# Attention, then a mixture of experts: the experts' rows in turns of 768 and 256 instead of 512 and 512

## The chip, the core and the metric

The kernel runs on one core of a Trainium2 chip. The core has five engines with an instruction queue each: PE (matrix multiplications), DVE (vector work), ACT (activation functions and copies), POOL (here above all the issuer of gathers and scatters by row number) and SP (issuer of plain transfers). Each queue is worked off in order; an instruction that has to wait holds all that stands behind it in its queue. Sixteen DMA engines move data between the large memory (HBM) and the core's own memory. [...]

The metric is the device time of one execution in microseconds (us). Twelve runs of the kernel before took 1091.36 to 1098.12 us, 1096.07 us in the median.

## What is computed

The input is x, 4 batches of 1024 rows of 256 numbers. The layer is causal attention with 16 heads, a layer norm, a mixture of experts, and another layer norm. The attention takes the first two thirds of the time and is not touched by the change. The part that matters, from the reference:

```python
scores = (jnp.einsum('btd,ed->bte', x, router_w) + router_b) / temp
gates = _sinkhorn(scores)                  # three rounds over experts and over rows of a batch
topk_vals, topk_idx = jax.lax.top_k(gates, K)          # K = 2 of E = 8 experts
topk_gates = topk_vals / (jnp.sum(topk_vals, axis=-1, keepdims=True) + 1e-08)
g = jax.nn.relu(jnp.einsum('btd,edf->btef', x, wg))    # 256 -> 512
p = jnp.einsum('btd,edf->btef', x, wp)                 # 256 -> 512
all_out = jnp.einsum('btef,efd->bted', g * p, wo)      # 512 -> 256
...
x = _layernorm(x + expert_out)
```

Each row goes to two experts, so there are 8192 pairs of a row and an expert, 1024 for each expert on average. The normalisation of the gates runs over all rows of a batch: who goes where in a batch is known only when the attention of the whole batch is done.

## The kernel before, in words

**Lists of pairs.** The kernel computes each pair only for the expert that wants it. After the attention of a batch, `finish` writes its normed rows to `x1_rows` in HBM (and, as the start of the sum, to `results`), and `route` works out gates and experts: many small steps on DVE, ACT and PE, one after the other. Then `route` scatters the pairs into a list in HBM, `pairs`, with 16 indirect transfers of 128 pairs on POOL (L842). The list has a region of `REGION` entries for each expert; an entry holds the row number, the row to add to, and the gate. `base` holds for each expert where its next pair goes. After the third batch of four, `base` is raised to `floor` where it is below it (L826), the end of the expert's first slot: what comes after it in the region is from then on pairs of the last batch, or pairs beyond the first slot.

**Slots.** A slot is a number of list entries of one expert that are worked on together. There are 8 first slots of ER = 512 entries (`Slot(0, e)`), 8 second slots of 512 (`Slot(1, e)`, in reverse order), and further slots of SR = 256 entries for what an expert has beyond 1024. How many further slots are needed, and where they lie, is worked out on the chip (`lay_out`); `SURE` = 3 of them are always run, and a branch runs all others when more than 3 are needed. Empty entries point to spare rows. The first slots need only pairs and rows of three batches (`x1_rows[: BT - T]`), so they can start, and be worked on, while the last batch is still being routed.

**One slot.** `gather` fetches the rows of a slot with one indirect transfer for 128 rows on POOL (L950), into one of two `xg` buffers. [...] `weights` loads three matrices of 512 KB from SP (L970) into one buffer each, and `halves` splits them with six copies on ACT (L190) and six subtractions on DVE (L191), into one of two buffers. `slot` then makes four blocks of gate and lin (`gp`, `lp`), each of 128 hidden columns, applies relu and product (L1006, L1007), splits the hidden block (`hh`, `hl`) and multiplies it with the third matrix into `eo`, 128 rows at a time. ACT copies `eo` out with the gate as scale (L1023) into one of six buffers, and POOL adds it to `results` with an indirect transfer (L1024). Two slots may hold the same row, so every add of a slot waits until all adds of the slot before it have landed (`after`, `added`). The second turn begins with the expert that the first turn ended with, and takes its split weights (`like`).

**The order.** `begin(keys, n, ...)` is a generator with the preparation of slot n: gathers for slot n + 1, `rows` for slot n, and three steps of `halves` and the next slot's `weights`; `slot` advances it between its blocks, so that slot n is prepared while slot n - 1 is computed. These instructions, and the small steps of the last batch's `route`, are then ordered within each engine's queue by a planner that the framework runs at build time. `begin_early` puts the first slot's loads ahead of the end of the attention.

**After the experts.** `results` is loaded again in 8 pieces (L1229), normed by DVE, POOL and ACT, and stored (L1232).

Of the kernel before, what the change touches and what calls it, by code (L numbers as in the profile page):

```python
# [14 lines left out]
ALU = mybir.AluOpType  # L15
# [11 lines left out]
SURE = 3  # L27
# [8 lines left out]
P = 128  # L36
# [7 lines left out]
def kernel(  # L44
# [38 lines left out]
    ER = 512  # L83
    SR = 256
    REGION = BT + SR
    NOVER = (2 * BT - 4 * ER + 2 * (SR - 1)) // SR
    NLIST = (E - 1) * REGION + 2 * ER + NOVER * SR
    NLIST += -NLIST % P

# [407 lines left out]
    for e in range(E):  # L497
        nc.gpsimd.memset(rank[:, e : e + 1], float(E - e))
        nc.gpsimd.memset(base[:, e : e + 1], float(e * REGION))
        nc.gpsimd.memset(floor[:, e : e + 1], float(e * REGION + ER))  # L500
    ones = const.tile([P, P], F32, name="ones")
# [354 lines left out]
    for e in range(E):  # L856
        nc.gpsimd.memset(shift[:, e : e + 1], float(e * REGION + 2 * ER - SR + 1))
    tables = {}

    def lay_out():  # L860
# [31 lines left out]
        nc.vector.scalar_tensor_tensor(table[:, 1], slot_no, float(SR), table[:, 1], ALU.mult, ALU.add)  # L892
        nc.vector.tensor_scalar(table[:, 1], table[:, 1], float(2 * ER), None, ALU.add)
        tables["slots"] = small.tile([1, 2, NOVER], I32, tag="ti", name="ti", bufs=1)
# [21 lines left out]
    class Slot:  # L916


        def __init__(self, which, s):
            self.which, self.s, self.name = which, s, f"{which}_{s}"  # L920
            self.rows = SR if which == 2 else ER
            self.blocks = self.rows // P
            self.raw, self.hl = [None] * 3, [None] * 3
            self.like = None

    lists = {}

    def pairs_of(k):
        if k.which == 2:
            row = value(1, k.s, NLIST - SR)  # L930
            k.ent = const.tile([P, k.blocks, 4], I32, name=f"ent_{k.name}")
            nc.sync.dma_start(
                out=k.ent, in_=pairs[bass.ds(row, SR)].rearrange("(p j) w -> p j w", j=k.blocks)
            )
            return
        if k.which not in lists:
# [3 lines left out]
                out=ent.rearrange("p e j w -> p e (j w)"),  # L940
                in_=regions[:, k.which * ER : (k.which + 1) * ER].rearrange("e (p j) w -> p e (j w)", p=P),
            )
            if not k.which:
                apart("pairs", "early", ins, ("last",))
        k.ent = lists[k.which][:, k.s]

    def gather(k):
        k.xg = early.tile([P, ER // P, C], F32, tag="xg", name=f"xg{k.name}", bufs=XG)
        for j in range(k.blocks):
            ins = nc.gpsimd.indirect_dma_start(  # L950
                out=k.xg[:, j], out_offset=None, in_=x1_rows[: BT if k.which else BT - T],
                in_offset=bass.IndirectOffsetOnAxis(ap=k.ent[:, j, 0:1], axis=0),
            )
            if not k.which:
                in_turn(ins)
                apart("x1", "early", ins, ("last",))

    def weights(k, i):

        if k.like is not None:  # L960
            return
        if k.which == 2:
            if i == 0:
# [8 lines left out]
    def halves(k, i):  # L972
        if k.like is not None:
            k.hl[i] = k.like.hl[i]
            return
        w = k.raw[i]
# [15 lines left out]
    def slot(k, between):  # L992

        R = k.rows
        hs = []
        for f in range(NFC):
            cut = slice(f * P, (f + 1) * P)
            if 2 * R > QC:
                gate, lin = (mx_tile(f"{i}p{k.name}_{f}") for i in "gl")
            else:  # L1000
                both = mx_tile(f"gp{k.name}_{f}")
                gate, lin = both[:, :R], both[:, R:]
            for (h_, l_), ps in zip(k.hl, (gate, lin)):
                mm3(ps, [(h_[:, c, cut], l_[:, c, cut], k.xh[:, c, :R], k.xl[:, c, :R]) for c in range(CC)])
# [9 lines left out]
        mine = []  # L1014
        h_, l_ = k.hl[2]
        for j in range(k.blocks):
# [11 lines left out]
            apart(f"results{k.name}", "add", ins, ("add",))  # L1028
            if not k.which:
                apart("results", "early", ins, ("last",))  # L1030
# [64 lines left out]
    budget = {0: (8.0, 8.0, 8.0, 11.3), 1: (9.5, 9.5, 6.0, 11.3), 2: (9.5, 9.5, 6.0, 0.0)}  # L1095
    first = [Slot(0, e) for e in range(E)]
    second = [Slot(1, e) for e in reversed(range(E))]
    second[0].like = first[-1]
    further = [Slot(2, n) for n in range(NOVER)]
    early = None  # L1100

    def begin_early():
        pairs_of(first[0])
        for i in range(3):
# [98 lines left out]
    def run(keys, given=()):  # L1203
# [4 lines left out]
    run(first + second + further[:SURE], (0,))  # L1208

# [133 lines left out]
```

## Time and profile before

| what | value |
|---|---|
| median of 12 runs | 1096.07 us (1091.36 to 1098.12) |
| the profiled execution | 1102.4 us, of which its span is 1100.7 us |
| PE busy | 985.3 us, 90% of the span, 6392 matmuls |
| DVE busy | 736.7 us, 67% |
| ACT busy | 626.2 us, 57% |
| POOL busy | 481.5 us, 44% |
| moved by DMA | 119.66 MB, 109 GB/s on average |
| first slot's rows transposed | from 721 us |
| last matmul of the experts | 1065 us |
| reload of `results` begins | 1075 us |

The profile is one execution. A line of a window gives start and end, its length, and then for PE, PEld (the loading of weights into PE), DVE, ACT and POOL the busy us with the number of instructions, the clock that PE was granted (1.00 is full speed), the share of time in which the DMA engines were busy, and GB/s. A line of the timeline gives start, duration, engine, line of the code, operation, tile written <- tiles read, size and count, and in brackets how long the engine had been idle and what ended that. Matmuls overlap, so the distance from one start to the next is what a matmul costs, not its duration. "remote" in such a bracket is a wait whose end the profile gives to no instruction of this core, as with transfers by POOL. The chain of waits gives start, length and what it was, followed back from the last instruction.

### The profile page before, as it was taken

To read this page: it belongs to the slowest core of one execution; us is meant where nothing else is said; L and a number is where in the kernel's file an instruction comes from. 1 tells how busy PE (TensorE), PEld (TensorE's weight loads), DVE (VectorE), ACT (ScalarE), POOL (GpSimd) and SP (SyncE) were. 2 spreads that over 40 slices of the span, in tenths; PEclk is the share of its full clock that TensorE was granted. 3 is DMA by queue.
4 is the path that set the end of the run, shared out by engine and by line. 5 is a ranking of instruction groups with operands and counts; after the bars stand their busy time and mean duration, and the time that the engine had idled before them with its cause. 6 is when DMAs were issued, how large, how long until landed. Compare 5 with 4: busy or idle time off the path is not lost.

```text
span 1100.7 us, 18000 instructions
## 1 busy us (share of the span) xinstructions
PE 985.3 (90%) x6392; PEld 606.9 (55%) x6392; DVE 736.7 (67%) x1630; ACT 626.2 (57%) x1314; POOL 481.5 (44%) x551
## 2 busy tenths in 40 slices
PE   6689999999999898999899799899999699999960
PEld 4455433455535244544345333278888488888860
DVE  3777787888888586788438688275676355646636
ACT  3455766765665564676566467665654354656633
POOL 6176511122443623351423301754566865653544
PEclk9899999999999898999999899999999699999985
DMA  6573420231230321323133220166573545665647
GB/s 237 167 221 116 116 98 19 63 116 57 75 115 31 93 69 49 125 66 109 50 97 105 45 63 2 21 214 167 111 177 74 122 89 151 137 152 108 155 61 305
DMA packets 71362, 119.66 MB, mean 109 GB/s; under 512 B 16416, under 2 KB 43040, under 8 KB 70880
## 3 DMA queue, kind: packets, MB, share of 16 engines
q1 hardware_dynamic: 48544, 81.76, 23.4%
q0 software_dynamic: 20672, 36.41, 15.3%
q8 instruction: 52, 0.85, 0.3%
q10 hardware_dynamic: 2048, 0.27, 0.2%
q14 instruction: 46, 0.38, 0.1%
HBM read 82.52 MB, written 35.60 MB: 107 GB/s over the span
## 4 chain that ended last, share of the span: by engine, by line
PE 74%; DVE 6%; ACT 6%; DMA 5%; issue 3%; SPq 2%; another core or an unknown queue 2%; POOL 1%; ACTq 0%; DVEq 0%; POOLq 0%
PE y L437 13%; PE s L353 11%; PE sT L456 10%; PE gp L198 3%; PE gp L199 3%; PE gp L197 3%; PE eo L197 3%; PE eo L198 3%; ACT pT L462 3%; PE eo L199 3%; PE lp L199 2%; PE lp L198 2%; PE lp L197 2%; PE po L623 2%; PE s L370 2%
## 5 line engine op out<-in xcount | busy, mean ns | idle before, releaser
L462 ACT ACTIVATE pT<-sT 128x512 f32<-128x512 f32 (+1 forms) x608 | 326.7, 576 | 184.2 <-PE sT L456 135.8
L374 DVE TENSOR_REDUCE mx<-s 128x1 f32<-128x384 f32 (+3 forms) x352 | 216.4, 632 | 63.3 <-PE s L370 45.4
L456 PE MATMUL sT<-qs,ks 98*128 98x512 bf16 (+3 forms) x768 | 216.1, 333 | 26.8 <-ACT pT L462 17.4
L353 PE MATMUL s<-ks,qs 96*128 96x512 bf16 (+3 forms) x768 | 213.0, 333 | 14.2 <-DMA ks<-parts 7.7
L474 POOL TENSOR_SCALAR_AFFINE_SELECT pT<-pT 128x512 f32<-128x512 f32 x120 | 75.8, 637 | 289.8 <-ACT pT L462 267.0
L383 DVE TENSOR_REDUCE mx<-s 128x1 f32<-128x512 f32 x256 | 171.0, 679 | 36.8 <-PE s L353 34.7
L437 PE MATMUL y<-pT,va 128*32 128x512 f32 (+3 forms) x1536 | 177.5, 510 | 3.0 <-issue 2.2
L1024 POOL DMA_INDIRECT results<-eo,ents x64 | 104.4, 1632 | 91.8 <-ACT eo L1023 68.9
L353 PEld LDWEIGHTS <-qs 96*128 96x128 bf16 x768 | 71.4, 100 | 123.3 <-issue 96.1
L456 PEld LDWEIGHTS <-ks 98*128 98x128 bf16 x768 | 69.5, 99 | 98.5 <-issue 65.4
L197 PE MATMUL eo<-wh,hh 128*128 128x256 f32 x280 | 81.9, 294 | 6.5 <-ACT eo L1023 6.5
L370 PE MATMUL s<-mask,ident_b 128*128 128x128 bf16 (+2 forms) x352 | 87.5, 249 | 0.0
L191 DVE TENSOR_TENSOR wl<-w,wh 128x512 fp32r<-128x512 f32 x108 | 69.6, 683 | 26.5 <-ACT wh L190 18.6
L1007 DVE TENSOR_TENSOR relu<-relu,lp 128x512 f32<-128x512 f32 x64 | 43.7, 683 | 64.7 <-PE lp L199 24.6
L842 POOL DMA_INDIRECT pairs<-ent,so_i x64 | 66.8, 1043 | 33.1 <-issue 18.1
L198 PE MATMUL eo<-wl,hh 128*128 128x256 f32 x280 | 80.2, 288 | 0.0
L1006 ACT ACTIVATE relu<-gp 128x512 f32<-128x512 f32 (+1 forms) x76 | 42.8, 563 | 65.7 <-PE gp L199 39.9
L950 POOL DMA_INDIRECT xg<-x_rows,ents x64 | 65.4, 1021 | 31.7 <-issue 17.4
L199 PE MATMUL eo<-wh,hl 128*128 128x256 f32 x280 | 78.0, 285 | 0.0
L437 PEld LDWEIGHTS y<-pT,va 128*32 128x32 f32 x1536 | 32.5, 109 | 68.4 <-issue 54.0
L191 DVE TENSOR_TENSOR hl<-relu,hh 128x512 fp32r<-128x512 f32 (+1 forms) x76 | 48.5, 645 | 29.1 <-ACT hh L190 19.9
L197 PE MATMUL gp<-xh,wh 128*128 128x512 f32 (+1 forms) x176 | 64.2, 371 | 3.3 <-DVE relu L1007 1.8
(212 smaller groups left out, 1852.0 us busy)
## 6 DMA issues: line engine op xcount, KB each, us to landing
ks<-parts SPq DMA_DIRECT2D x90, 128.0 KB
w<-in_wg_dram SPq DMA_DIRECT2D x18, 512.0 KB
w<-in_wp_dram SPq DMA_DIRECT2D x18, 512.0 KB
w<-in_wo_dram SPq DMA_DIRECT2D x18, 512.0 KB
qs<-parts SPq DMA_DIRECT2D x66, 128.0 KB
parts<-lv POOLq DMA_DIRECT2D x12, 384.0 KB
parts<-lv POOLq DMA_DIRECT2D x24, 192.0 KB
xh<-in_x_t_dram SPq DMA_DIRECT2D x8, 512.0 KB
```

Source lines behind the costliest of these rows:

```text
L191: (sub or nc.vector).tensor_tensor(lo, src, hi.bitcast(F32), ALU.subtract)
L197: nc.tensor.matmul(ps, lhsT=sh, rhs=mh, start=(i == 0), stop=False)
L198: nc.tensor.matmul(ps, lhsT=sh, rhs=ml, start=False, stop=False)
L199: nc.tensor.matmul(ps, lhsT=sl, rhs=mh, start=False, stop=(i == n - 1))
L353: nc.tensor.matmul(ps, lhsT=q(h, half)[:NROW, t * P : (t + 1) * P], rhs=k(h, kc)[:NROW, :w], start=first, stop=last,)
L370: nc.tensor.matmul(each[:, :, w - P :], lhsT=ident_b, rhs=mask.unsqueeze(1).to_broadcast([P, m, P]), start=False, stop=True,)
L374: nc.vector.tensor_reduce(mx_of[:, half, h0 : h0 + m, t], each, AX.X, ALU.max)
L383: nc.vector.tensor_reduce(mx_of[:, kc, h, t : t + 1], ps, AX.X, ALU.max)
L437: nc.tensor.matmul(acc[g, qc][SLOT * h : SLOT * (h + 1), lo:], lhsT=va[b % 2][:, kb, at : at + SLOT], rhs=pT[:, h, lo:], start=(kb == 0), ...
L456: nc.tensor.matmul(st[:, h % m * w : (h % m + 1) * w], lhsT=k(h, kb // BPQ)[: NROW + 2, kb % BPQ * P : (kb % BPQ + 1) * P], rhs=q(h, qc)[: ...
L462: nc.scalar.activation(pT[:, h + 1 - m : h + 1, lo:], st[:, : m * w].rearrange("p (h t) -> p h t", t=w), AF.Exp, scale=scale,)
L1024: ins = nc.gpsimd.indirect_dma_start(out=results[:, :], out_offset=bass.IndirectOffsetOnAxis(ap=k.ent[:, j, 1:2], axis=0), in_=eo, in_offs ...
```

## The change

The regions of the list, the slots and their order change; the mathematics and the number of pairs don't.

- The first turn takes 768 entries of each expert, as two slots: `Slot(0, e)` with entries 0 to 511 and `Slot(1, e)` with entries 512 to 767. The second of them has `like` set to the first and uses its split weights. Both draw on the rows of three batches only.
- The second turn takes 256 entries, 768 to 1023, as `Slot(2, e)`, in reverse order of the experts. The first of these uses the weights of the last expert of the first turn, as before.
- The further slots are `Slot(3, n)`, 256 entries as before, beyond 1024.
- `floor` is raised from entry 512 to entry 768 of each region. `FIXED`, the number of entries in the fixed slots, is 1024 as `2 * ER` was.
- `pairs_of` loads a list for each of the three kinds of fixed slots. Two of them are loaded early, `begin_early` does so for the first two slots.
- `begin` gathers for the next slot in all cases, and looks for the next slot with weights of its own: its `halves` are made in the slot before it, unless they are there already, and the weights after that are loaded.

In all there are 8 slots of 512 and 16 of 256 entries, and 3 further ones, where there were 16 of 512 and 3 further ones. [...]

```diff
+    FIXED = ER + 2 * SR
     REGION = BT + SR
-    NOVER = (2 * BT - 4 * ER + 2 * (SR - 1)) // SR
-    NLIST = (E - 1) * REGION + 2 * ER + NOVER * SR
+    NOVER = (2 * BT - 2 * FIXED + 2 * (SR - 1)) // SR
+    NLIST = (E - 1) * REGION + FIXED + NOVER * SR
...
-        nc.gpsimd.memset(floor[:, e : e + 1], float(e * REGION + ER))
+        nc.gpsimd.memset(floor[:, e : e + 1], float(e * REGION + ER + SR))
...
-            self.rows = SR if which == 2 else ER
+            self.at, self.rows = ((0, ER), (ER, SR), (ER + SR, SR), (None, SR))[which]
...
-                in_=regions[:, k.which * ER : (k.which + 1) * ER].rearrange("e (p j) w -> p e (j w)", p=P),
-            )
-            if not k.which:
+                in_=regions[:, k.at : k.at + k.rows].rearrange("e (p j) w -> p e (j w)", p=P),
+            )
+            if k.which < 2:
                 apart("pairs", "early", ins, ("last",))
...
     def weights(k, i):
-        if k.like is not None:
-            return
...
     def halves(k, i):
-        if k.like is not None:
-            k.hl[i] = k.like.hl[i]
-            return
...
+        hl = (k.like or k).hl
...
-    first = [Slot(0, e) for e in range(E)]
-    second = [Slot(1, e) for e in reversed(range(E))]
-    second[0].like = first[-1]
-    further = [Slot(2, n) for n in range(NOVER)]
+    first = [Slot(which, e) for e in range(E) for which in range(2)]
+    for a, b in zip(first[::2], first[1::2]):
+        b.like = a
+    second = [Slot(2, e) for e in reversed(range(E))]
+    second[0].like = first[-2]
+    further = [Slot(3, n) for n in range(NOVER)]
...
     def begin_early():
-        pairs_of(first[0])
+        for k in first[:2]:
+            pairs_of(k)
...
         k, nxt = keys[n], keys[n + 1] if n + 1 < len(keys) else None
-        early_next = nxt is not None and (nxt.which == 0 or k.which > 0)
-        if n not in given and (k.which and (n == 0 or not keys[n - 1].which)):
+        if n == 0 and not given:
             pairs_of(k)
             gather(k)
-        if early_next:
-            pairs_of(nxt)
+            for i in range(3):
+                weights(k, i)
+        if nxt is not None:
+            if nxt.ent is None:
+                pairs_of(nxt)
             gather(nxt)
-        if n not in given:
-            if n == 0:
-                for i in range(3):
-                    weights(k, i)
+        if n or not given:
             rows(k, st_tile)
+        own = [m for m in keys[n:] if m.like is None][:2]
         for i in range(3):
-            halves(k, i)
-            if nxt is not None:
-                weights(nxt, i)
+            if own and own[0].hl[i] is None:
+                halves(own[0], i)
+                if len(own) > 1:
+                    weights(own[1], i)
             yield
```

More of the change, by code (lines that the diff above doesn't have):

```diff
@@ L856 @@
     for e in range(E):
-        nc.gpsimd.memset(shift[:, e : e + 1], float(e * REGION + 2 * ER - SR + 1))
+        nc.gpsimd.memset(shift[:, e : e + 1], float(e * REGION + FIXED - SR + 1))
     tables = {}
@@ L892, in lay_out @@
         nc.vector.scalar_tensor_tensor(table[:, 1], slot_no, float(SR), table[:, 1], ALU.mult, ALU.add)
-        nc.vector.tensor_scalar(table[:, 1], table[:, 1], float(2 * ER), None, ALU.add)
+        nc.vector.tensor_scalar(table[:, 1], table[:, 1], float(FIXED), None, ALU.add)
         tables["slots"] = small.tile([1, 2, NOVER], I32, tag="ti", name="ti", bufs=1)
@@ L920, in __init__ @@
             self.which, self.s, self.name = which, s, f"{which}_{s}"
-            self.rows = SR if which == 2 else ER
+            self.at, self.rows = ((0, ER), (ER, SR), (ER + SR, SR), (None, SR))[which]
             self.blocks = self.rows // P
             self.raw, self.hl = [None] * 3, [None] * 3
+            self.ent = None
             self.like = None
@@ L928, in pairs_of @@
     def pairs_of(k):
-        if k.which == 2:
+        if k.which == 3:
             row = value(1, k.s, NLIST - SR)
@@ L950, in gather @@
             ins = nc.gpsimd.indirect_dma_start(
-                out=k.xg[:, j], out_offset=None, in_=x1_rows[: BT if k.which else BT - T],
+                out=k.xg[:, j], out_offset=None, in_=x1_rows[: BT - T if k.which < 2 else BT],
                 in_offset=bass.IndirectOffsetOnAxis(ap=k.ent[:, j, 0:1], axis=0),
             )
-            if not k.which:
+            if k.which < 2:
                 in_turn(ins)
@@ L958, in weights @@
     def weights(k, i):
-        if k.like is not None:
-            return
-        if k.which == 2:
+        if k.which == 3:
             if i == 0:
@@ L1002, in slot @@
                 gate, lin = both[:, :R], both[:, R:]
-            for (h_, l_), ps in zip(k.hl, (gate, lin)):
+            for (h_, l_), ps in zip(hl, (gate, lin)):
                 mm3(ps, [(h_[:, c, cut], l_[:, c, cut], k.xh[:, c, :R], k.xl[:, c, :R]) for c in range(CC)])
@@ L1014, in slot @@
         mine = []
-        h_, l_ = k.hl[2]
+        h_, l_ = hl[2]
         for j in range(k.blocks):
@@ L1028, in slot @@
             apart(f"results{k.name}", "add", ins, ("add",))
-            if not k.which:
+            if k.which < 2:
                 apart("results", "early", ins, ("last",))
@@ L1184, in begin, with run @@
         k, nxt = keys[n], keys[n + 1] if n + 1 < len(keys) else None
-        early_next = nxt is not None and (nxt.which == 0 or k.which > 0)
-        if n not in given and (k.which and (n == 0 or not keys[n - 1].which)):
+        if n == 0 and not given:
             pairs_of(k)
             gather(k)
-        if early_next:
-            pairs_of(nxt)
+            for i in range(3):
[3 more added lines that the diff above has]
+                pairs_of(nxt)
             gather(nxt)
-        if n not in given:
-            if n == 0:
-                for i in range(3):
-                    weights(k, i)
+        if n or not given:
             rows(k, st_tile)
+        own = [m for m in keys[n:] if m.like is None][:2]
         for i in range(3):
-            halves(k, i)
-            if nxt is not None:
-                weights(nxt, i)
+            if own and own[0].hl[i] is None:
+                halves(own[0], i)
+                if len(own) > 1:
+                    weights(own[1], i)
             yield
-    def run(keys, given=()):
+    def run(keys, given=False):
         drain(begin(keys, 0, given))
@@ L1206, in run @@
             slot(key, begin(keys, n + 1, given))
-    run(first + second + further[:SURE], (0,))
+    run(first + second + further[:SURE], True)
     experts.close()
```

## The prediction

> **What bounds the kernel now.** I read the page's busy shares first (PE 90% of 1100.7 us), then, since the change touches only the experts, windows over the expert stage, the timeline across its one hole, and POOL's and SP's queues. As built, the two programs agree on every engine up to the first transposes of gathered rows at 721 us, so only what follows can move. The windows (PE, PEld, DVE, ACT, POOL busy; then granted clock, DMA share, GB/s):
>
> ```profile
> 835.00:857.00 22.00, 20.26 (x119) 16.89 (x117) 10.54 (x21) 8.51 (x18) 17.43 (x16) 1.00 0.28 75
> 857.00:866.00 9.00, 2.47 (x10) 2.00 (x9) 1.98 (x3) 2.55 (x6) 7.17 (x7) 0.63 0.43 67
> 866.00:876.00 10.00, 7.17 (x23) 5.62 (x24) 4.47 (x7) 3.27 (x7) 8.47 (x6) 0.50 0.90 226
> ...
> 900.00:937.00 37.00, 37.00 (x217) 32.50 (x217) 20.33 (x32) 19.63 (x39) 19.18 (x16) 1.00 0.56 128
> ...
> 1030.00:1040.00 10.00, 9.98 (x83) 9.73 (x81) 6.46 (x14) 5.81 (x15) 3.47 (x3) 1.00 0.68 199
> ```
>
> PE is full in both turns and in the further slots (1030 on). The hole is 835 to 876: 1.74 + 6.53 + 2.83 = 11.1 us of idle PE, and about 9.6 busy us at half clock, worth 4.8 us more: **15.9 us** in all. The timeline says whose hole it is:
>
> ```profile
> 856.47 0.96 POOL L842 DMA_INDIRECT pairs<-ent,so_i  x1 [0.30 <-issue]
> 857.73 1.93 POOL L1024 DMA_INDIRECT results<-eo,ents  x1 [0.30 <-issue]
> 858.82 0.37 SPq L939 DMA_DIRECT2D ents<-pairs  x1
> ...
> 862.55 0.47 ACT L1023 ACTIVATE eo<-eo,ents 128x256 f32<-128x256 f32 x1 [5.11 <-remote]
> ...
> 863.08 0.58 PE L197 MATMUL eo<-wh,hh 128*128 128x256 f32 x1 [5.90 <-ACT eo L1023]
> ...
> 864.89 0.37 SPq L970 DMA_DIRECT2D w<-in_wo_dram  x1
> ```
>
> From 833.89 to 857.43 POOL issues the last batch's sixteen scatters of pairs (23.5 us), with the adds of results queued behind them. All six `eo` buffers fill, ACT's copy waits until the first delayed add has landed (857.73 to 862.55, 4.8 us), and PE waits for ACT. SP stands at the load of `ents` from 840 to 858.8, so no weights arrive either.
>
> **The change, part by part.** *The sizes.* I counted the pairs of each expert with the reference on its inputs: 719, 701, 714, 777, 783, 739, 912, 799 from three batches, and 233, 236, 231, 243, 268, 256, 307, 274 from the last. With a floor of 512 or of 768, three experts pass 1024 and need one further slot each, so three further slots run in both kernels. Rows (8960) and weight loads (18 of each matrix) stay. Eight 512-row slots become sixteen of 256.
>
> *Narrower matmuls, on the path.* PE's timeline, start to start:
>
> ```profile
> 1023.03 0.39 PE L197 MATMUL gp<-xh,wh 128*128 128x512 f32 x1
> 1023.25 0.39 PE L198 MATMUL gp<-xl,wh 128*128 128x512 f32 x1
> ...
> 1031.93 0.28 PE L198 MATMUL gp<-xl,wh 128*128 128x256 f32 x1
> 1032.05 0.28 PE L199 MATMUL gp<-xh,wl 128*128 128x256 f32 x1
> ```
>
> A 512-wide matmul takes 0.228 us, a 256-wide one 0.120. A 512-row slot has 48 of them for gate and lin; two slots of 256 have 96: 48 x (0.240 - 0.228) = 0.56 us, times 8 = **+4.5 us**. The output matmuls (256 wide before, too) and the transposes keep their number. ACT and DVE get some 80 instructions more each and run beside PE.
>
> *The hole, smaller but not gone.* In POOL's built queue the sixteen scatters now stand behind the gather for the 512-row slot of expert 4 and before the adds of expert 2's 256-row slot; the route's last matmuls come some 18 us of PE work earlier, so the offsets are ready. The wait is counted from the moment PE has transposed expert 3's 512 rows, which frees the gather's buffer: 1.6 us until POOL is free, 4 gathers x 1.28 (start to start), 16 scatters x 1.265 (20.2, or 23.5 as at 833.89), 2 adds x 1.87, and about 3 us until the first block of expert 4's 256-row gather, which now stands behind those adds, has landed: 33.7 to 37 us. PE's queue holds 31.3 us of matmuls before it transposes that block (its instructions times the durations above). Idle: 2.4 to 6 us, and 0.8 more for the second block; I take 5. Expert 6's weights are also held behind `ents`, but are needed over 30 us later. By windows of 2 and 3 us the clock fell to 0.50 after 2.2 us of idle PE (857.1 to 859.3) and came back after 5.9 us of dense work (870.5 to 876.4); the same again costs 2.9 us. So 7.9 us stay and the hole gives back **-8 us** (ends: -12.7, with 3.2 us idle and the clock kept; 0, if it only moves).
>
> [...]
>
> *The route's chain*, now packed closer: its steps stand in PE's queue in 46 us of work rather than 58, and PE waits where DVE and ACT are late. The pure chain of the third round took 17 us from 796.9 to 814 with slot work between; 12 are left. No row shows the denser order. Ends 0 (before, PE never waited there) and +4 (a microsecond at each of four steps); I take **+1.5**.
>
> *The second turn at 256 rows.* A slot is 72 x 0.120 + 4 x 0.11 = 9.1 us of PE instead of 17.6 (17.86 measured: the same add of every second slot starts at 937.13, 972.85, 1008.58). But each still brings three weight matrices and twelve half splits. Per slot: ACT 7.3 and DVE 7.1 us by the rows at 1030 to 1060, both hidden. DMA: in 900 to 937 queue 1 took 21.6% for 5 loads (1.6 us each) and queue 0 33.8% for 16 gathers and adds (0.78 each), so 3 x 1.6 + 4 x 0.78 = 7.9 of 9.1 us, 87%, where now it is 11.0 of 17.86. POOL is closest: each slot's adds wait until the previous slot's have landed. The chain of waits shows what that takes:
>
> ```profile
> 1062.69 4.09 DMA results<-eo,ent
> 1066.84 0.69 issue
> 1067.53 6.75 DMA results<-eo,ent
> ```
>
> 4.09 + 0.69 = 4.8 us from an add to the next slot's. In the built queue the gathers (2 x 1.28) stand between a slot's two adds, not behind them where they would cover the landing: 1.87 + 2.56 + 4.8 = 9.2 us a slot, the same as PE. Two queues of equal length with six `eo` buffers and two `xg` buffers between them lose a little. The nearest row is the three further slots of 256, where PE lost 2.1 us more than its matmuls explain, 0.7 a slot, against 0.25 for 512 rows. Over 8 slots, 0.6 each: **+5 us**. Ends: 0 (1030 to 1040 is full), and +16, if an add lands 1.9 us later under the heavier load (11.1 us a slot).
>
> [...]
>
> *Where nothing changes.* The end (last adds, reload, norm) follows the same three further slots. SP gets one load of `ents` more, before 721 us; the 256-row slots with borrowed weights issue none.
>
> **Sum:** 4.5 - 8 + 1.5 + 5 = +3.0 us on the profiled 1102.4 (span 1100.7). That execution is 6.3 us above the median of the runs, so I put the difference on the median: 1096.07 + 3.0 = 1099.1.
>
> **The rivals.** *(a) Faster: the scatters are covered.* If the first scatters are not long (20.2 us) and a gather lands in 2 us, POOL needs 32.7 us, and PE waits 1.4 + 0.8 = 2.2 us and keeps its clock. Deciding point: some 33 us on POOL against PE's 31.3. With a second turn at PE's pace: -13 + 4.5 + 0.5 + 1 = -7, 1089. For it: the 1030 row. Against: scatters of 1.48, 2.59 and 2.38 us at 833.89 to 838.58. *(b) Clearly slower: POOL or DMA sets the second turn.* At 11 us a slot, ACT's in-order queue blocks on `eo` or weights, PE idles in each slot: +16 in place of +5, sum +14, 1110. For it: 87% DMA and 9.2 against 9.1. Against: 8 us of lead that each gather has. *(c) The change isn't what it says:* expert 5 ends at exactly 1024 rows (768 + 256). One pair more makes four further slots, and the branch then runs all 22 remaining: 22 x 9.1, about 1300 us. The nearest token's gates differ by 0.5%, so 1 in 100.
>
> **How the numbers follow.** Forecast 0.47 (1094 to 1105), (a) 0.34, (b) 0.18, (c) 0.01. A measurement of this kernel tells 0.2%, 2.2 us, from no change: the forecast's own spread gives 0.13 within it and 0.02 below, the rest above. Faster 0.36, same 0.13, slower 0.51. For 8 in 10 the range must take in most of (a) and (b): 1087 to 1111.
>
> **What would show it.** The hole: one idle of PE of 3 to 7 us after the sixteen scatters, ended by the transposes of `xg` and not by `eo`, with some 6 us at half clock; if it is gone, (a). The second turn: adds of one slot to the next every 9.1 (PE), 9.7 (mine) or 11 us (b), POOL idle until results have landed, ACT waiting at `wh` if weights are late. 256-wide gp spaced 0.120. PE waits at the route's small matmuls. Most wrong would be the length of the last scatters and the landing time under load, which no row shows.

## The result, and the profile after

The changed kernel took 1116.64 us in the median of 15 runs (1111.70 to 1126.13); the kernel before, run beside it, 1097.80 us (62 runs). The ratio is 1.0174, with a 95% interval of 1.0157 to 1.0192: **slower by 18.8 us**, where 3.0 were forecast. The time lies above the whole range (1087 to 1111). The profiled execution took 1120.34 us, with a span of 1118.5 us. PE was busy for 994.9 us of it (89%), with 6776 matmuls, 384 more than before.

The windows of the changed kernel, with the same columns as before:

```profile
830.00:840.00 10.00, 3.38 (x10) 2.07 (x10) 0.00 (x0) 0.60 (x1) 7.56 (x9) 0.75 0.03 2
840.00:850.00 10.00, 3.30 (x11) 2.79 (x12) 1.78 (x3) 1.00 (x2) 5.56 (x5) 0.50 0.39 59
850.00:860.00 10.00, 9.55 (x66) 9.03 (x66) 6.03 (x14) 7.38 (x17) 4.86 (x3) 0.89 0.39 105
...
890.00:920.00 30.00, 29.55 (x198) 26.82 (x197) 15.59 (x28) 16.95 (x37) 17.89 (x15) 1.00 0.51 115
...
1000.00:1020.00 20.00, 19.95 (x167) 19.75 (x167) 15.82 (x36) 15.01 (x39) 10.26 (x8) 1.00 0.83 229
...
1040.00:1050.00 10.00, 8.07 (x65) 7.66 (x64) 6.20 (x15) 6.28 (x16) 6.29 (x5) 1.00 0.68 140
1050.00:1060.00 10.00, 7.95 (x67) 7.75 (x65) 5.56 (x12) 6.10 (x15) 4.42 (x4) 1.00 0.73 198
```

Three things differ from the forecast. The hole (830 to 850) is no smaller than the one before: 13.3 us of idle PE. The second turn (1000 to 1020) is full, 19.95 of 20 us, at a DMA share of 0.83: the 5 us forecast there are not lost there. The further slots (1040 to 1060), which were full before, lose 2 us in 10.

The hole, in the timeline of the same kernel:

```profile
829.98 0.19 PEld L200 LDWEIGHTS gp<-xh,wl 128*128 128x128 f32 x1 [0.51 <-issue]
830.68 0.19 PEld L199 LDWEIGHTS gp<-xl,wh 128*128 128x128 f32 x1 [0.40 <-issue]
831.39 0.28 PE L199 MATMUL gp<-xl,wh 128*128 128x256 f32 x1 [0.91 <-issue]
832.08 0.19 PEld L200 LDWEIGHTS gp<-xh,wl 128*128 128x128 f32 x1 [1.21 <-issue]
...
840.56 0.69 DVE L1005 TENSOR_TENSOR relu<-relu,lp 128x512 f32<-128x512 f32 x1 [12.73 <-remote]
```

PE is not waiting for any one thing here. It advances in steps of 0.70 us (829.98, 830.68, 831.39, 832.08), mostly one instruction at a time, in the middle of the gate and lin blocks of a slot whose rows and weights have long been there, and each wait is put down to "issue". DVE stands still for 12.73 us with "remote". In the later profile of the kernel before, shown below, full `eo` buffers show as one wait of 4.16 us with a releaser; this does not look like that.

The further slots, first in the chain of waits and then in the timeline:

```profile
1037.14 6.08 DMA w<-in_wg_dram
...
1048.63 5.73 DMA results<-eo,ents
...
1058.72 3.61 DMA xg<-x_rows,ent
```

```profile
1026.45 9.34 SPq L970 DMA_DIRECT2D w<-in_wo_dram  x2
1036.30 0.34 SPq L934 DMA_DIRECT2D ent<-pairs  x1
1037.14 0.37 SPq L970 DMA_DIRECT2D w<-in_wg_dram  x1
...
1043.30 0.62 ACT L191 CAST wh<-w 128x512 fp32r<-128x512 f32 x1 [3.66 <-DMA w<-in_wg_dram]
1044.24 0.50 PE L198 MATMUL gp<-xh,wh 128*128 128x256 f32 x2 [1.64 <-ACT wh L191]
```

The chain now runs through a load of weights. The row of 9.34 us holds two loads, one at 1026.45 and one that ends at 1035.79. SP's queue stands for some 8.6 us at the second, the third matrix of the first further slot, whose buffer is not free yet; the list (1036.30) and the next slot's first matrix (1037.14) stand behind it, and ACT and PE wait for that matrix at 1043 and 1044.

### The profile page after: what moved, and what is told of

Its sections match the earlier page's. It is cut to its first block, busy times and chain, and to the rows that moved or that the text cites. A ratio compares the mean times of both kernels' runs of the same rounds, so it can differ in the third digit from the quotient of the medians.

```text
span 1118.5 us, 18958 instructions
## 1 busy us (share of the span) xinstructions
PE 994.9 (89%) x6776; PEld 633.1 (57%) x6776; DVE 749.1 (67%) x1710; ACT 640.0 (57%) x1394; POOL 478.9 (43%) x551
## 4 chain that ended last, share of the span: by engine, by line
PE 73%; DVE 6%; ACT 6%; DMA 5%; issue 5%; SPq 2%; POOL 1%; another core or an unknown queue 1%; ACTq 0%; DVEq 0%; POOLq 0%
PE y L438 13%; PE s L354 11%; PE sT L457 10%; PE gp L199 4%; PE gp L198 4%; PE gp L200 4%; ACT pT L463 3%; PE eo L198 3%; PE eo L199 2%; PE eo L200 2%; PE po L624 2%; PE s L371 2%; SPq L339 2%; DVE mx L384 2%; DVE mx L375 1%
## 5 line engine op out<-in xcount | busy, mean ns | idle before, releaser
L463 ACT ACTIVATE pT<-sT 128x512 f32<-128x512 f32 (+1 forms) x608 | 326.7, 575 | 181.1 <-PE sT L457 132.3
L199 PE MATMUL gp<-xl,wh 128*128 128x256 f32 (+1 forms) x368 | 115.4, 315 | 3.2 <-issue 3.2
L198 PE MATMUL gp<-xh,wh 128*128 128x256 f32 (+1 forms) x368 | 112.1, 311 | 4.8 <-issue 3.1
L200 PE MATMUL gp<-xh,wl 128*128 128x256 f32 (+1 forms) x368 | 112.2, 306 | 2.7 <-issue 2.7
L1004 ACT ACTIVATE relu<-gp 128x256 f32<-128x256 f32 (+1 forms) x108 | 48.2, 447 | 53.4 <-PE gp L200 39.6
L191 ACT CAST hh<-relu 128x256 fp32r<-128x256 f32 (+1 forms) x108 | 49.8, 471 | 49.1 <-DVE relu L1005 47.1
L843 POOL DMA_INDIRECT pairs<-ent,so_i x64 | 63.5, 991 | 33.1 <-issue 18.7
```

The costliest lines, as they stand in the source:

```text
L198: nc.tensor.matmul(ps, lhsT=sh, rhs=mh, start=(i == 0), stop=False)
L199: nc.tensor.matmul(ps, lhsT=sh, rhs=ml, start=False, stop=False)
L200: nc.tensor.matmul(ps, lhsT=sl, rhs=mh, start=False, stop=(i == n - 1))
L463: nc.scalar.activation(pT[:, h + 1 - m : h + 1, lo:], st[:, : m * w].rearrange("p (h t) -> p h t", t=w), AF.Exp, scale=scale,)
```

## Both kernels again, in later runs

All ratios from here on are to the kernel before on the same chip. On the four chips of the later runs (2, 4, 5 and 11) that kernel took 1055.88 to 1057.08 us in the median, some 41 us less than in the first set, whose chip is not on record. So one profile of each kernel was taken again, unaltered: the changed kernel's on chip 2, that of the kernel before on chip 4.

> The changed kernel unaltered, for a second profile of it. In the first one PE went from 829.2 to 849.1 us through one instruction each 0.70 us, with no wait shown ('issue'), in the middle of the last batch's sixteen scatters and past their end. If that stall belongs to the scatters or to this place of PE's program, it stands here too, within a few us of the same place and about 15 us worth, and the ratio is 1.017 to the kernel before. If it was an accident of one execution, it is gone from this profile, and the span is some 12 us shorter.

> The kernel before, unaltered, for its profile on the chip of this call. Its hole after the scatters was 15.9 us in the first profile, with PE stopped by eo for 5.9 us. In the second profile of the changed kernel the hole was 9.6 us. If the change made the hole smaller by the 8 us of the prediction, 14 to 17 us stand here. If the hole differs as much from one execution to the next as from one kernel to the other, it is well under 14 here too, and then the prediction's gain of 8 us was never there.

*Measured.* The changed kernel 1080.25 us, ratio 1.0229 (1.0202 to 1.0256), span 1078.6. The kernel before 1058.19 us in this run, span 1056.5. The code is the same, so the n-th matmul of one profile can be set against the n-th of the other, and its lag says where the first profile of the kernel before lost its 44.2 us of span:

| between (us, first profile of the kernel before) | scatters on POOL from | lag grows from | to | by |
|---|---|---|---|---|
| 366 and 395 | 367 | -2.0 | 6.1 | 8.1 |
| 414 and 445 | 415 | 6.1 | 13.3 | 7.2 |
| 533 and 565 | 535 | 13.3 | 21.2 | 7.9 |
| 611 and 640 | 613 | 22.0 | 31.7 | 9.8 |
| 683 and 740 | 684 | 31.7 | 32.8 | 1.1 |
| 833 and 876 | 834 | 32.8 | 49.1 | **16.3** |
| 885 and 890 | none | 49.1 | 45.2 | -3.9 |

Ahead of 366 us the lag drifts between -2.2 and 1.0. From there on, outside of these stretches, it stays within 0.1 us for most of the time (0.75 at the most). In the first set's profile five of the six rows of scatters set PE back by 7 us or more, and at the row from 684 the lag rose by 4.6 us and fell again; in the later one no row did this. At the last row the lag begins to grow some 16 us after the first scatter. The 15.9 us that I had read as a full `eo` buffer are this stop, and all of it: ACT's copy of `eo`, which I had waiting for a delayed add until 862.55, is in the later timeline of the kernel before this one (the instructions ahead of it on ACT are the same, one for one):

```profile
818.74 0.48 ACT L1023 ACTIVATE eo<-eo,ents 128x256 f32<-128x256 f32 x1 [0.33 <-PE eo L199]
...
825.40 1.61 POOL L1024 DMA_INDIRECT results<-eo,ents  x1 [0.30 <-issue]
```

It ran 6.7 us before the first delayed add was even issued, so its buffer was free, and no add can have ended its 5.11 us of "remote" in the first set. The queue's own hole comes later, and is the -3.9 of the table: in the first set PE was by then so late that it didn't have to wait there. The changed kernel gives the same picture, with a lag that grows by 19.0 at its last row and falls by 9.4 where its own hole is due. What the queues alone make of it is seen in the second profiles. Of the kernel before, windows and two lines of the timeline:

```profile
830.00:841.00 11.00, 8.96 (x53) 7.68 (x52) 3.46 (x6) 3.97 (x9) 8.56 (x8) 1.00 0.80 213
841.00:851.00 10.00, 10.00 (x56) 8.81 (x56) 4.19 (x7) 4.24 (x10) 8.17 (x7) 0.83 0.67 137
```

```profile
839.12 0.47 ACT L1023 ACTIVATE eo<-eo,ents 128x256 f32<-128x256 f32 x1 [4.16 <-DMA results<-eo,ents]
839.64 0.38 PE L197 MATMUL eo<-wh,hh 128*128 128x256 f32 x1 [2.04 <-ACT eo L1023]
```

Here a copy of `eo` does wait for a delayed add, and PE for the copy: the mechanism that I had given for the hole before, three copies later than I had it. It costs 2.04 us of idle and 1.7 of half clock: 3.7 us. Of the changed kernel, timeline, then windows:

```profile
813.67 0.95 POOL L843 DMA_INDIRECT pairs<-ent,so_i  x1 [0.30 <-issue]
814.93 1.60 POOL L1022 DMA_INDIRECT results<-eo,ents  x1 [0.30 <-issue]
...
818.71 1.01 POOL L952 DMA_INDIRECT xg<-x_rows,ents  x1 [0.30 <-issue]
819.15 0.47 ACT L1021 ACTIVATE eo<-eo,ents 128x256 f32<-128x256 f32 x1 [5.09 <-DMA results<-eo,ents]
...
824.51 0.45 PE L986 MATMUL xgT_ps<-ident,xg 128*128 128x128 f32 x1 [6.64 <-DMA xg<-x_rows,ents]
```

```profile
810.00:818.00 8.00, 7.68 (x48) 6.58 (x48) 3.52 (x7) 3.05 (x8) 6.48 (x6) 1.00 0.16 14
818.00:832.00 14.00, 7.49 (x29) 6.50 (x30) 3.69 (x6) 4.31 (x9) 9.02 (x7) 0.63 0.63 137
```

That is the forecast's own mechanism, line for line: the last scatter, the adds behind it, the gather behind the adds, and PE waiting for `xg` for 6.64 us.

The whole difference, in windows of 2 us from the 4381st matmul, the same one in both kernels and 4 to 11 us ahead of the first transpose of gathered rows, to the end of the last slot. A loss is idle PE, plus busy time times the missing share of the clock; "work" is what remains:

| part | before, later profile | after, later profile | difference | difference in the first set |
|---|---|---|---|---|
| start (first 20 us) | 5.5 | 8.5 | +3.0 | +3.1 |
| hole | 3.7 | 9.5 | +5.7 | +1.6 (15.6 to 17.2) |
| short waits | 1.5 | 2.5 | +1.0 | +1.0 |
| further slots | 1.2 | 6.5 | +5.3 | +7.6 |
| work of PE | 326.7 | 332.5 | +5.8 | +7.2 |
| length | 338.8 | 359.7 | +20.9 | +20.6 |

The spans differ by 22.1 and 17.8 us. In the later pair the rest lies ahead, in the attention: the 4381st matmul came 1.3 us later in the changed kernel's profile. In the first set it came 4.7 us earlier, and what follows the last slot took 1.9 us longer. In the later profiles of all kernels this matmul starts between 677.8 and 682.8 us, so spans and times of single executions carry some 5 us from outside the experts; the length leaves that out. All differences but the short waits were then tried one by one.

## The hole: scatters spread out

`after_spread` takes the last batch's sixteen scatters out of their row. Each goes behind an add of the first turn's later slots, once that add has landed; `after_hold` does the same and puts 18 power operations of POOL, about 20 us of it, where the scatters had stood. (These kernels' lines are up to 20 further down.)

```diff
+        if b == B - 1:
+            held.extend((scatter, n, k) for n in range(NB) for k in range(2))
+            return
...
+            if k.which < 2 and k.s >= 4:
+                for put, *at in held[:1]:
+                    after(put(*at), ins)
+                del held[:1]
```

> The changed kernel with the last batch's sixteen scatters taken apart: from the adds of expert 4 on, each add of the first turn is followed by one scatter, in place of all sixteen in a row. Nothing else moves. Theory 'supply' (the burst of scatters makes PE's own instructions come late) and theory 'buffers' (the one of the prediction: POOL is held, adds and gathers come late, PE runs out of eo or xg) both expect the hole to go: 15 to 18 us less than the changed kernel, ratio 0.999 to 1.004 against the kernel before. Theory 'place' (PE's program at this point, narrow matmuls, whatever POOL does) expects the 0.70 us stall to remain and the time within 4 us of the changed kernel, ratio 1.014 to 1.018.

> The spread kernel, and at the place of the old burst POOL is held for some 20 us by nineteen small arithmetic instructions (128x4, 1.05 us each) that move no data, ahead of the same adds and gathers. 'Buffers' expects the hole back: PE waits with a releaser shown (xg or eo), 5 to 16 us over the spread kernel. 'Supply' by scatters expects no instruction at 0.70 us and at most 4 us over the spread kernel. If POOL's arithmetic alone slows PE's supply, the 0.70 us stall is back.

*Measured.* `after_spread` 1079.14 us, ratio 1.0214 (1.0178 to 1.0249): no gain over the changed kernel's 1.0229. `after_hold` 1088.62 us, 1.0292 (1.0263 to 1.0322). In `after_spread` the hole is gone, but the loss has moved to the second turn's list, in the timeline:

```profile
914.69 0.37 SPq L949 DMA_DIRECT2D ents<-pairs  x1
...
918.92 0.99 POOL L960 DMA_INDIRECT xg<-x_rows,ents  x1 [3.53 <-issue]
...
921.84 0.45 PE L994 MATMUL xgT_ps<-ident,xg 128*128 128x128 f32 x1 [4.23 <-DMA xg<-x_rows,ents]
```

The spread scatters end at about 913.5, the list can be loaded only then, and 7.8 us are lost between 911 and 931. In `after_hold` a POOL that is merely busy makes a hole of 6.4 us, which ends by `eo`, and no instruction of PE is spaced by 0.70 us:

```profile
823.92 0.58 PE L198 MATMUL eo<-wh,hh 128*128 128x256 f32 x1 [3.67 <-ACT eo L1031]
```

It also made the list late: it is loaded at 925.19, PE waits 6.68 us for the first gather behind it, and 10.1 us are lost between 925 and 939. Two more waits for gathers (2.34 us at 897.81, and 6.47 us at 1034.19 in the further slots) lost 4.2 and 6.9. So a blocked POOL queue is enough for a hole of this kind, here of 6.4 us. It could not show what the first set's stop is, since on its chip the scatters did not stop PE either.

Two scatters behind each add, in order but without waiting for it to land, end sooner; the kernel before was given the same.

```diff
-                for put, *at in held[:1]:
-                    after(put(*at), ins)
-                del held[:1]
+                for put, *at in held[:2]:
+                    behind_of(put(*at), ins)
+                del held[:2]
```

> The changed kernel with its sixteen scatters two by two behind eight adds, and no wait for those adds to land. One behind each of sixteen adds was too slow: the scatters ended at 913 us and the load of ents behind them came 12 us too late for the second turn, which cost what the hole had cost. Now the scatters end some 40 us earlier: no hole at the scatters and none at the second turn, 9 to 15 us less than the changed kernel, ratio 1.009 to 1.014 to the kernel before. If POOL has no room for them anywhere in the first turn, a new wait of over 3 us at xg shows, and the ratio stays at 1.017 to 1.023.

> The kernel before with its last batch's sixteen scatters taken apart: two behind each of the eight adds of experts 4 and 5. If the row of sixteen makes the hole, 9 to 16 us go, ratio 0.985 to 0.992. If PE's stop at this place comes from something else, ratio 0.998 to 1.002.

*Measured.* `after_spread2` 1071.61 us, 1.0145 (1.0116 to 1.0174), without a hole and with the list in time: 0.0084 of 1056, some 9 us, below the changed kernel, against the 9.5 of the table. In its profile the 9.5 are gone, while the start and other waits lose 2.4 more. `before_spread2` 1066.49 us, 1.0106 (1.0080 to 1.0132): 11 us worse. Its first turn is shorter and wants the list at its end. In its timeline POOL, then PE, wait for that list:

```profile
840.28 0.97 POOL L965 DMA_INDIRECT xg<-x_rows,ents  x1 [5.28 <-DMA ents<-pairs]
...
843.20 0.45 PE L1004 MATMUL xgT_ps<-ident,xg 128*128 128x128 f32 x1 [8.62 <-DMA xg<-x_rows,ents]
```

So the longer first turn does buy time for the last batch's list. As changed, the kernel has no use for it: the scatters stay in one row, and it is the gather behind them that is late.

## The hole: which buffer ends it

If the hole of the changed kernel is ended by the gather, a third `xg` buffer lets that gather stand ahead of the scatters; if by full `eo` buffers, eight of them instead of six help.

```diff
-XG = 2
+XG = 3
```

```diff
-EO = 6
+EO = 8
```

> The changed kernel with three gather buffers for two. In POOL's queue the gather of expert 4's 256 rows now stands ahead of the scatters, not behind them and two adds. If that gather makes the hole (the prediction's mechanism), 5 to 9 us go there, and part of the 2.4 us at the last further slot's transposes: ratio 1.013 to 1.018 where the changed kernel has 1.023. If eo makes it too, ACT's wait for eo (5.09 us) stops PE a little later and 2 us or less go: 1.020 to 1.023.

> The changed kernel with eight eo buffers for six, POOL's queue as it was. If xg makes the hole, PE still waits 6 to 7 us for the gather and the time stays within 2 us: ratio 1.020 to 1.024. If eo makes it, 5 us or more go.

> The kernel before with three gather buffers. Its hole of 3.7 us is ended by eo, so nothing should move there: ratio 0.998 to 1.001. If its gathers too are late, up to 3 us less, 0.997.

*Measured.* `after_xg3` 1068.37 us, 1.0103 (1.0058 to 1.0148), some 13 us below the changed kernel by the ratios; `after_eo8` 1082.74 us, 1.0254 (1.0204 to 1.0304), none. The windows of `after_xg3` across the place of the hole, and the timeline of `after_eo8`:

```profile
800.00:832.00 32.00, 31.55 (x221) 29.16 (x220) 17.33 (x32) 18.41 (x40) 25.90 (x21) 1.00 0.51 106
```

```profile
820.79 0.45 PE L986 MATMUL xgT_ps<-ident,xg 128*128 128x128 f32 x1 [6.35 <-DMA xg<-x_rows,ents]
```

With the third `xg` buffer 0.45 us are lost where 9.5 were; with more `eo` buffers PE waits for the same gather, 6.35 us. By the table's measure the further slots of `after_xg3` lose 9.3 us instead of 6.5, so its gain in the experts is the hole's alone, and the length falls by 5.9 us. The two spans differ by 9.7, of which 4.2 lie ahead of the 4381st matmul: the 13 us of the ratios are not all the buffer's. For the kernel before a third buffer is no gift: 1061.52 us, 1.0039 (1.0021 to 1.0057), its hole 8.6 us instead of 3.7.

## The end: SP's order

`after_tail` loads a slot's own matrix if it is not there yet, and does not load the third matrix of a further slot ahead of time, so that SP does not stand at it.

```diff
+                if own[0].raw[i] is None:
+                    weights(own[0], i)
                 halves(own[0], i)
-                if len(own) > 1:
+                if len(own) > 1 and not (i == 2 and own[1].which == 3):
                     weights(own[1], i)
```

`after_both2` has this and the scatters of `after_spread2`.

> The changed kernel with SP's order altered at the three further slots only: the third weight matrix of each is loaded behind the first two of the next slot, as SP does it by itself in the second turn, in place of ahead of them. If the 8 us that PE lost at 1040 to 1080 come from weights that stand in SP's queue behind a load that waits for its buffer, the waits of ACT's wh for wg (3.66 and 2.84 us) go and the time falls by 5 to 9 us, ratio 1.009 to 1.013. If the further slots are held by POOL's adds (4.8 us from an add to the next slot's), it stays within 2 us of the changed kernel.

> The kernel of the last run with SP's order at the further slots altered as well (third weight matrix behind the first two of the next slot). If the two losses are independent, 4 to 5 us less than the last run, ratio 1.004 to 1.010. What then remains over the kernel before with its scatters spread is what the change costs without the hole and without SP's order: by the prediction 4.5 for narrower matmuls, 5 for the second turn and 1.5 for the route, 11 us.

*Measured.* `after_tail` 1075.95 us, 1.0161 (1.0120 to 1.0202), 4.3 us below the changed kernel on the same chip by the medians and 7.2 by the ratios, though the intervals of the two just touch. Forecast were 5 to 9. ACT's waits for `w` are gone, and the loss in the further slots is 3.7 us instead of 6.5; the length in its profile falls by 2.1 us, since the start lost 1.0 more than in the changed kernel, and other parts differ a little. What is left is mainly a gather that stands behind an add:

```profile
1010.33 0.33 PE L986 MATMUL xgT_ps<-ident,xg 128*128 128x128 f32 x1 [2.32 <-DMA xg<-x_rows,ent]
```

The add was issued at 1000.80 and the gather at 1004.23, and PE had its rows 6.1 us after that; the DMA engines were busy for 0.99 of the time from 1006 to 1010. How much of it is the queue's and how much the landing's, no run shows.

`after_both2` 1067.66 us, 1.0101 (1.0068 to 1.0135), 4 us below `after_spread2`: the two repairs add up, as far as intervals that overlap can say.

## The start: two stores ahead of a gather

In the changed kernel the first rows that PE transposes are those of expert 0's slot of 256. Its gather stands on POOL behind the two stores of the last normed block. Timeline of the changed kernel, later profile:

```profile
684.56 0.85 POOL L652 DMA_DIRECT2D x_rows<-x  x1
685.39 0.82 POOL L656 DMA_DIRECT2D results<-x  x1
686.51 1.48 POOL L952 DMA_INDIRECT xg<-x_rows,ents  x1 [0.30 <-issue]
...
692.89 0.69 PE L986 MATMUL xgT_ps<-ident,xg 128*128 128x128 f32 x2 [4.80 <-DMA xg<-x_rows,ents]
```

and of the kernel before, where a 512-row slot's gathers were issued ahead of the stores:

```profile
683.59 0.95 POOL L950 DMA_INDIRECT xg<-x_rows,ents  x1 [0.30 <-issue]
...
686.42 0.30 PE L989 MATMUL xgT_ps<-ident,xg 128*128 128x128 f32 x1 [1.33 <-DMA xg<-x_rows,ents]
...
687.04 0.83 POOL L651 DMA_DIRECT2D x_rows<-x  x1
```

`after_start` issues the last batch's stores from SP:

```diff
-            store = nc.sync if alone else nc.gpsimd
+            store = nc.sync if b == B - 1 else nc.gpsimd
```

> The changed kernel, with the last batch's two stores of 512 KB (its first half of x_rows and of results) on SP's queue in place of POOL's, where they stood between the gather of expert 0's 512 rows and that of its 256 rows. PE's first transposes are those of the 256-row slot, and they waited 4.8 us for that gather. If this queue order is what the change lost at its start (8.5 us of idle and half clock against 5.5 before), the wait goes and 2 to 5 us with it, ratio 1.018 to 1.021 to the kernel before where the changed kernel has 1.023. If the gather is late because the DMA engines are full with weights, it stays within 1 us of the changed kernel.

*Measured.* 1078.10 us, 1.0203 (1.0183 to 1.0223), 0.0026 or 2.7 us below the changed kernel by the ratios, whose intervals overlap. The profile tells more. Its timeline:

```profile
683.63 0.95 POOL L952 DMA_INDIRECT xg<-x_rows,ents  x1 [0.30 <-issue]
685.19 0.30 PE L986 MATMUL xgT_ps<-ident,xg 128*128 128x128 f32 x1 [1.33 <-DMA xg<-x_rows,ents]
...
686.46 0.33 PE L986 MATMUL xgT_ps<-ident,xg 128*128 128x128 f32 x1 [0.97 <-DMA xg<-x_rows,ents]
```

PE's wait of 4.80 has become 1.33 + 0.97, and the loss at the start 5.7 instead of 8.5.

On POOL the two stores took 0.85 + 0.82 us to issue, and PE got back 2.5 of its wait (4.80 less 1.33 and 0.97). The saving was larger than the issue time alone. But the stores also ran earlier: in `after_start` SP issues them at 675.40 and 675.82, some 9 us ahead of where they stood, and PE has the gather's first rows 2.8 us after POOL began to issue it, where it was 6.4. No run here tells whether this came from the order in a queue or from DMA engines that were by then done with the stores.

## Narrower matmuls by themselves

`before_narrow` is the kernel before with the second turn's gate and lin made in two halves of 256 columns; nothing else changes.

```diff
-                mm3(ps, [(h_[:, c, cut], l_[:, c, cut], k.xh[:, c, :R], k.xl[:, c, :R]) for c in range(CC)])
+                for a in range(0, R, SR if k.which else R):
+                    z = slice(a, a + (SR if k.which else R))
+                    mm3(ps[:, z], [(h_[:, c, cut], l_[:, c, cut], k.xh[:, c, z], k.xl[:, c, z]) for c in range(CC)])
```

> The kernel before, with the gate and lin matmuls of its second turn taken in two halves of 256 rows, in the same slots, with the same weights, gathers and adds: the 384 more matmuls of the change and nothing else of it. The prediction's term for the narrower matmuls is +4.5 us; the work of PE in the two second profiles differs by 5.8. Expected ratio 1.004 to 1.006. If ACT, DVE or POOL set the pace there and not PE, 0.999 to 1.002.

*Measured.* 1065.59 us, 1.0086 (1.0065 to 1.0106), that is 9.1 us. By the table's measure PE's work grows by 5.5 us (326.7 to 332.2), and the length by 8.7. Windows across the second turn, of the kernel before and of `before_narrow`:

```profile
862.00:982.00 120.00, 119.27 (x703) 104.45 (x702) 66.44 (x106) 66.88 (x132) 73.19 (x55) 1.00 0.64 147
```

```profile
870.00:990.00 120.00, 117.05 (x963) 115.33 (x963) 63.96 (x100) 65.09 (x126) 68.63 (x50) 1.00 0.57 135
```

Idle PE in 120 us went from 0.73 to 2.95 us; the remaining microsecond is spread. The work term is the whole of what the changed kernel's PE has more to do (5.8), within 0.3 us.

## All repairs together

`after_all` has the scatters of `after_spread2`, the end of `after_tail` and the stores of `after_start`; `after_all_xg3` the third `xg` buffer besides. `before_best` gives the kernel before the stores on SP and eight `eo` buffers.

> The changed kernel with all three repairs: scatters two by two, SP's order at the further slots, stores on SP's queue. If the losses add up, 3 us less than the kernel with the first two (1.010), so 1.006 to 1.009: the narrower matmuls alone, with 1 or 2 us of short waits.

> The changed kernel with the three repairs and three gather buffers. What it then keeps over the kernel before is the narrower matmuls (5.5 us of PE work) less the hole that the kernel before still has (3.7): ratio 1.002 to 1.005. Below 1.000 it would beat the kernel before.

> The kernel before with the stores on SP's queue and eight eo buffers for six. In its second profile PE lost 3.7 us behind the scatters, waiting 2.04 us for eo, and 5.5 us at the start, 2.2 of it waiting for gathers. If eo and the queue are the causes, 3 to 6 us less, ratio 0.994 to 0.997; otherwise 0.999 to 1.001.

*Measured.* `after_all` 1063.23 us, 1.0054 (1.0034 to 1.0074). `after_all_xg3` 1058.31 us, 1.0018 (0.9998 to 1.0039). `before_best` 1058.75 us, 1.0018 (1.0003 to 1.0033): no gain; the start got worse by 2.2, and its hole stayed 3.7 us with eight `eo` buffers. The wait for `eo` is gone there, and PE waits 1.97 us for the gather behind the adds instead.

Windows across the second turn's end and the further slots of `after_all_xg3`:

```profile
988.00:1019.00 31.00, 30.04 (x246) 29.28 (x244) 18.74 (x43) 18.96 (x49) 14.25 (x10) 1.00 0.49 109
```

0.96 us is lost where the changed kernel lost 6.5. By the table's measure this kernel stops for 8.1 us in all, against 12.1 of the kernel before, and works 6.4 us longer: 2.4 us more, where the times say 1.9. With the hole, the loss in the further slots and the late gather at the start taken away, the 4 us of stops that this version saves, in part by repairs that have nothing to do with the change, are less than what PE works longer. No version was faster than the kernel before; this one can't be told from it.

## Why the prediction was wrong

**The direction was right, the size was not:** +18.8 in the first set and +24 in the later runs (0.0229 of 1056), against +3.0. Step by step:

- *Narrower matmuls, +4.5.* Mechanism right, mis-sized: 5.8 in the later pair, and 5.5 by `before_narrow`, or 0.0143 us for each of the 384 additional matmuls instead of the 0.012 that I read from spacings rounded to 0.01. The first pair has 7.2. In `before_narrow` the narrow form brought some 3 us of waits besides, which the step had put down as hidden.
- *The hole, -8.* **This step failed.** It was +5.7 in the later pair, +1.6 in the first set. What I worked out for the hole after was right where nothing else stops PE: PE waits for `xg` behind the adds behind the scatters, 5 us of idle and 2.9 of half clock forecast, 6.5 and 2.8 measured between 818 and 832 of the later profile, and `after_xg3` and `after_eo8` show that it is `xg` and not `eo`. What was wrong was the hole *before*: "all six `eo` buffers fill, ACT's copy waits until the first delayed add has landed". The add landed at about the right moment, and I took that for the cause. The copy did not need it; the 15.9 us were a stop at this row of scatters (16.3 by the lag), with that buffer free. A hole by full `eo` buffers does exist, three copies later, and it was worth 3.7. The profile had the signs: the wait was "remote", not one for a transfer of `results`, and the earlier rows of scatters, where no `eo` is in play, stopped PE, too (7 to 10 us each for four of them, by the lag). In the first set the stop was there again after the change, at the same scatters in their new place, 19.0 us by the lag in place of the 7.9 forecast.
- *Half clock, 2.9 of the 7.9.* The size came out by luck. That the clock falls after 2.2 us of idle and returns after 5.9 of dense work is no rule of these profiles: in the later one of the kernel before it fell 3.5 us after PE had stopped and was back after 3.4 (last section).
- *The route's chain, +1.5.* Nothing was seen. The +1.0 of short waits lies at the experts' transposes, 0.45 each.
- *The second turn at 256 rows, +5.* Not there: 0.05 us lost in 1000 to 1020, at the DMA share of 0.83 (0.87 forecast from the packets). The "nearest row" that I priced it by, the further slots, lost for a reason of their own.
- *"Where nothing changes."* **This step failed, too**, twice. The end "follows the same three further slots", but what precedes them is shorter: with slots of half the length, SP stands at the third matrix while the list and the next slot's weights are wanted, +5.3 to +7.6. And at the start, costed as "SP gets one load of `ents` more", the order on POOL changed: a 256-row slot's gather behind two stores, +3.0. I had looked past the first transposes of the second slot without following what each queue had ahead of its gather.

The account: 9.3 missed (3.0 + 5.3 + 1.0), 13.7 from the hole (-8 to +5.7) and 1.3 from the narrow term, less 6.5 forecast in vain (1.5 + 5), is 17.8; with the forecast's 3.0 that makes 20.8, the sum of the table's parts.

**The rivals.** (a), faster, needed scatters covered by PE's work, and PE waited 6.64 us instead of 2.2. That PE keeps its clock through 2.2 us, or through the 3.2 of the hole's better end, isn't shown either: the 2.04 us of the kernel before cost it 1.7 of half clock. The cover was tried in `after_spread2`, and even with the hole away the kernel is slower by 15 us. (b), 1110, came nearest in size, by another way: neither POOL nor DMA sets the second turn, which lost 0.05 us in 1000 to 1020. (c) did not happen; three further slots ran.

**What stays open** is the cause of the first set's stop. It was seen with rows of scatters only, in the two profiles of the first set and in none of the later ones, and whether the chip makes the difference is not known; PE, ACT and DVE are affected, while POOL's scatters mostly follow each other every 1.26 us in both. What lies between the scatters and these engines, no run shows. For the change itself it matters little: the kernel is slower by 18.8 us with it and by 24 without.

## What to carry to other kernels

Before a hole is credited to a full buffer, count which earlier use must have freed that buffer; and where a wait is put down to "issue" or "remote", look for the same operation elsewhere in the profile, where the supposed cause is missing. When a unit of work is halved, follow each in-order queue across the first and the last unit, where the steady state's cover is absent: here the two places costed at nothing brought 8 us, and the middle, which had been worked out at length, none. A longer cover for late work is only worth having if something in the queues can use it; here the gather's buffer, not the length of the turn, was what held.

## What was unexpected of the hardware

- One and the same program ran 41 us (4%) shorter in the later runs, on four chips, and nearly all of it lay in five short stretches at rows of scatters, with a lag constant to about 0.1 us over most of the rest; at the changed kernel's last row PE advanced in steps of 0.70 us.
- Two queues that were forecast to be as long as PE's (POOL 9.2 us a slot, DMA 87% busy) did not slow it: 256-row slots with their own weights ran with PE at 99.8% between 1000 and 1020.
- Half clock followed a wait of 2.04 us as well as one of 6.64, and not at one distance. In the later profile of the changed kernel the clock fell to 0.50 2.1 us after PE had stopped (817.9 to 820.0) and was back after 10.2, of which PE was at work for 5.6. In that of the kernel before it fell 3.5 us after PE had stopped, when PE had been working again for 1.5, and was back after 3.4, as the windows below show. So the wait of 2.04 us cost 1.7 us of half clock as well. The 5.9 us of dense work that I had counted were the last of 17.1 us at half clock (859.3 to 876.4 in the first profile of the kernel before).

```profile
839.60:841.10 1.50, 1.46 (x12) 1.46 (x13) 0.99 (x2) 1.50 (x4) 1.20 (x2) 1.00 0.49 70
841.20:844.50 3.30, 3.30 (x12) 2.71 (x11) 2.93 (x6) 2.38 (x5) 2.69 (x3) 0.50 0.67 76
```
